# One of two factored-attention batches moves from ahead of a cross attention into the work interleaved with it

## Chip, cores, metric

One core of one Trainium2 chip. The metric is the device time of the whole program in microseconds, the median of several runs. The engines are called PE (TensorE matmul), PEld (its weight load), DVE (VectorE), ACT (ScalarE), POOL (GpSimd) and SP (SyncE, which issues most DMAs).

## What is computed

A decoder of four layers on x of 8 batches, 256 tokens and width 128, with a context of 512 tokens a batch. Each layer adds an attention, a cross attention and a feed-forward part to x, each on the layer-normed x. The change touches the passage from layer 1's feed-forward part (L1_ffn) over layer 2's attention (L2_attn) to layer 2's cross attention (L2_xattn):

```python
x = x + L1_ffn(layernorm(x))
x = x + L2_attn(layernorm(x))
x = x + L2_xattn(layernorm(x), ctx)

def L2_attn(x):                       # 16 heads of width 8
    q, k, v = heads(x @ W_qkv + b_qkv)
    s = q @ k.T * scale
    s = where(fenwick_mask, s, -inf)  # a query sees the keys 0, 1, 2, 4, ... 128 tokens back
    return merge(softmax(s) @ v) @ W_proj + b_proj

def L2_xattn(q, kv):                  # 16 heads of width 8, 256 queries, 512 keys
    qh, kh, vh = heads(q @ Wq.T + bq), heads(kv @ Wk.T + bk), heads(kv @ Wv.T + bv)
    return merge(softmax(qh @ kh.T * scale) @ vh) @ Wo.T + bo

def L1_ffn(x):
    xr, xk = mix(x, previous token's x)
    return sigmoid(xr @ W_r.T) * (relu(xk @ W_k.T) ** 2 @ W_v.T)
```

## The kernel before

The kernel is written against a tile framework: a scheduler orders each engine's instructions by program order as priority and by its own idea of durations, and sets all waits. Only matmuls and transposes issued through the `_Heads` object (lines 451 and 454) keep strict program order among themselves on PE.

x lives in SBUF as 16 tiles of 128 tokens, two a batch; `E.xt(b)` is the layer-normed, transposed x of batch b.

**The factored attention** `_l2_attn` (L2_attn) works on one tile at a time, with a product per offset instead of a full score matrix. `weigh(t)` makes q (`fa_q`), for pairs of offsets keys and values (`fa_kvps`), the products (`fa_pr`, DVE), the value copies (`fa_v`, ACT), the softmax over offsets (`fa_sc`, `fa_red`), and the weighted values (POOL). `apply(t)` sums them (`fa_o`), transposes, multiplies by the output matrix (`fa_yps`), adds to x, and after the second tile of a batch norms that batch (`_norm`, `_normed`). It is a generator: each `yield` is the end of one step. A first tile's `weigh` has 5 steps and a second tile's 6; `apply` has 1 and 5. `through(g, n, ahead)` runs the tiles of n groups of four, `weigh(t)` before `apply(t - 1)`; `ahead(g)` is run before a group's first tile, and is a unit of L1_ffn (7 steps).

**The middle** `_middle` runs L0_ffn to L2_attn. L1_ffn's group 0 is done in its first part. Then comes, at its end, the passage of the change: `E.beginning` of the cross attention is advanced once (fills of the first head buffers on ACT, line 368; the key projection of batch 0, its spread by DMA, and the values); `_run(fa(0, 1))` runs tiles 0 to 3, that is batches 0 and 1; `E.beginning` is advanced again (the query projection `mh_qps` of batch 0, its copy `mh_qf` at line 417, its split `mh_qp` on POOL, eight SP DMAs that spread it over the heads, and the fills of the second head buffers). The rest, `rest()`, becomes the guest: tiles 4 to 15 with L1_ffn's groups 1 to 3 ahead of them, and then the preparation of L2_ffn's weights (10 steps).

**The cross attention** `_heads_attention` runs 128 heads (t, 16 a batch) in one loop. Head t's scores (`mh_sps`) and their maxima (`mh_nm`) are made at t, its exponentials (`mh_e`) 8 heads later, and every four heads are combined. At head 6 of a batch the next batch's keys are projected, at head 9 its queries; before that the loop makes sure that the next batch is normed:

```python
while h == (2 if causal else 9) and b + 1 not in normed_already:
    visit(1)
...
if guest:
    visit(pace(t))
```

`visit(rate)` adds to a credit and runs that many whole steps of the guest. `known` holds the batches normed before the loop begins. Two PSUM banks (`E.heads.g`) serve the guest and the attention's small matmuls.

Of the kernel before, what the change touches and what calls it, by code (L numbers as in the profile page):

```python
# [43 lines left out]
NT = B * S // P  # L44
# [162 lines left out]
def _normed(E, b, z, psum, turn_over=None):  # L207

    ps = psum.tile([P, 2, D], F32, tag="g", name="ln_ps")
    for q in range(2):  # L210
        if turn_over:
            turn_over(ps[:, q, :], z[:, q, :])
        else:
            E.nc.tensor.transpose(ps[:, q, :], z[:, q, :], E.ident)
    E.nc.scalar.copy(E.xt(b), ps.rearrange("p q t -> p (q t)"))  # L215
# [6 lines left out]
def _run(steps):  # L222
    for _ in steps:
        pass
# [544 lines left out]

def _l2_xattn(E, ctx):  # L770
    guest, E.guest = E.guest, None
    _heads_attention(E, ctx, guest=guest, known=(0, 1), pace=lambda t: 1.25)


def _l3_attn(E, ctx):
# [303 lines left out]
def _l2_attn(E, ctx):  # L1079


    nc, W = E.nc, E.w("L2_attn")
    wk = ctx.enter_context(E.tc.tile_pool(name="fa", bufs=2))
    scale = DH ** -0.5
    NO = len(OFFS)
    heads = lambda a: a.rearrange("p (h d) -> p h d", d=DH)
    st = {}

    def weigh(t):
        b, half = divmod(t, 2)  # L1090
        at = slice(half * P, half * P + P)
        if half == 0:
            E.pre_add(b, W("bo"))
        offs = [o for o in OFFS if o < P * (half + 1)]
        no = len(offs)
        ps = E.banks.fa.tile([P, D], F32, tag="g", name="fa_qps")
        E.mm(ps, E.xt(b)[:, at], W("wqkv")[:, :D], start=True, stop=True)
        q = wk.tile([P, D], F32, name="fa_q")
        nc.vector.tensor_tensor(q, ps, W("b")[:, :D], ALU.add)

        yield
        qb = wk.tile([P, D], F32, tag="fa_s", name="fa_qb")
        nc.gpsimd.tensor_tensor(qb, q, W("b")[:, D : 2 * D], ALU.mult)
        pr = wk.tile([P, NO, D], F32, name="fa_pr")
        v = wk.tile([P, NO, D], F32, name="fa_v")
        for i in range(0, no, 2):
            n = min(2, no - i)
            ps = E.banks.fa.tile([P, 2, 2 * D], F32, tag="g", name="fa_kvps")
            for j in range(n):
                E.mm(ps[:, j, :], E.xt(b, offs[i + j])[:, at], W("wqkv")[:, D:], start=True, stop=True)  # L1110
            nc.vector.tensor_tensor(
                pr[:, i : i + n, :], ps[:, :n, :D], q.unsqueeze(1).to_broadcast([P, n, D]), ALU.mult
            )
            nc.scalar.copy(v[:, i : i + n, :], ps[:, :n, D:])
            yield
        sb = wk.tile([P, H], F32, name="fa_sb")
        nc.vector.tensor_reduce(sb, heads(qb), AX.X, ALU.add)
        sc = wk.tile([P, NO, H], F32, name="fa_sc")
        a = sc[:, :no, :]
        nc.vector.tensor_reduce(a, pr[:, :no, :].rearrange("p o (h d) -> p o h d", d=DH), AX.X, ALU.add)  # L1120
        nc.vector.tensor_tensor(a, a, sb.unsqueeze(1).to_broadcast([P, no, H]), ALU.add)
        if half == 0:
            nc.vector.tensor_tensor(a, a, W("fenwick")[:, :no].unsqueeze(2).to_broadcast([P, no, H]), ALU.add)
        red = wk.tile([P, H], F32, name="fa_red")
        wide = red.unsqueeze(1).to_broadcast([P, no, H])
        nc.vector.tensor_reduce(red, a.rearrange("p o h -> p h o"), AX.X, ALU.max)
        nc.vector.tensor_tensor(a, a, wide, ALU.subtract)
        nc.scalar.activation(a, a, AF.Exp, scale=scale)
        nc.vector.tensor_reduce(red, a.rearrange("p o h -> p h o"), AX.X, ALU.add)
        nc.vector.reciprocal(red, red)  # L1130
        nc.vector.tensor_tensor(a, a, wide, ALU.mult)
        v4 = v[:, :no, :].rearrange("p o (h d) -> p o h d", d=DH)
        nc.gpsimd.tensor_tensor(v4, v4, a.unsqueeze(3).to_broadcast([P, no, H, DH]), ALU.mult)

        nc.gpsimd.tensor_tensor(v[:, :4, :], v[:, :4, :], v[:, 4:8, :], ALU.add)
        st[t] = v, no

    def apply(t):
        v, no = st.pop(t)
        o = wk.tile([P, D], F32, tag="fa_s", name="fa_o")  # L1140
        nc.vector.tensor_tensor(v[:, :2, :], v[:, :2, :], v[:, 2:4, :], ALU.add)
        nc.vector.tensor_tensor(o, v[:, 0, :], W("b")[:, 2 * D :], ALU.add)
        nc.vector.tensor_tensor(o, o, v[:, 1, :], ALU.add)
        if no > 8:
            nc.vector.tensor_tensor(o, o, v[:, 8, :], ALU.add)
        ps = E.banks.fa.tile([P, P], F32, tag="g", name="fa_tps")
        E.turn_over(ps, o)
        ot = wk.tile([P, P], F32, name="fa_ot")
        nc.scalar.copy(ot, ps)
        yield  # L1150
        ps = E.banks.fa.tile([P, D], F32, tag="g", name="fa_yps")
        E.mm(ps, ot, W("wo"), start=True, stop=True)
        nc.vector.tensor_tensor(E.x[:, t, :], ps, E.x[:, t, :], ALU.add)
        if t % 2:
            z = _norm(E, t // 2)
            yield
            yield
            yield
            _normed(E, t // 2, z, E.banks.ln, E.turn_over)
            yield t // 2  # L1160

    def through(g, n, ahead=lambda g: ()):

        first, end = 4 * g, 4 * (g + n)
        for t in range(first, end + 1):
            if t < end:
                if t % 4 == 0:
                    yield from ahead(t // 4)
                yield from weigh(t)
            if t > first:  # L1170
                yield from apply(t - 1)

    return through
# [8 lines left out]
def _middle(E, names, then):  # L1182

    nc = E.nc
    plain_pe(E)
    banks = lambda to, name, bufs, side="left": to.enter_context(
        E.tc.tile_pool(name=name, bufs=bufs, space=PSUM, side=side)
    )  # L1190
    if names != MIDDLE:
        for n in names:
            with ExitStack() as scope:
                pg = E.mid_ln = banks(scope, "mid_pg", 6)
                E.banks = SimpleNamespace(fa=pg, rk=pg, ln=pg)
                unit = {
                    "L0_ffn": _l0_ffn, "L1_attn": _l1_attn, "L1_xattn": _l1_xattn, "L1_ffn": _l1_ffn,
                    "L2_attn": _l2_attn,
                }[n](E, scope, *([pg] if n in MIDDLE[:3] else []))
                if n == "L2_attn":  # L1200
                    _run(unit(0, 4))
                    continue
                for g in range(4):
                    _run(unit(g) or ())
        E.close_weights()
        return
    last, psum, scope, early = (ExitStack() for _ in range(4))
    E.mid_ln = banks(psum, "mid_ln", 1)
    mid = banks(scope, "mid_pg", 4, "right")
    moe = _l0_ffn(E, scope, banks(early, "moe_pg", 3))  # L1210
    ra, xa = _l1_attn(E, scope, mid), _l1_xattn(E, scope, mid)
    rk = _l1_ffn(E, scope, "right")
    E.banks = SimpleNamespace(rk=mid, ln=E.mid_ln)
    for s in range(4):
        if s > 2:
            _run(rk(s - 3))
        if s > 1:
            xa(s - 2)
        if s:
            ra(s - 1)  # L1220
        moe(s)
    early.close()
    E.close_big()
    ra(3)
    xa(2)
    xa(3)
    scope.close()
    E.banks.fa = banks(psum, "fa_pg", 3)
    fa = _l2_attn(E, last)
    guest = then in HEADS  # L1230
    begun = E.beginning(then)
    if guest:
        next(begun)
    _run(fa(0, 1))
    if guest:
        next(begun, None)
    psum.close()

    def rest():
        if guest:  # L1240
            g = E.heads.g
            E.mm, E.turn_over, E.transpose = E.heads.mm, E.heads.turn_over, E.heads.transpose
            E.banks = SimpleNamespace(fa=g, rk=g, ln=g)
        with ExitStack() as own:
            if not guest:
                g = banks(own, "mid_pg2", 6)
                E.banks = SimpleNamespace(fa=g, rk=g, ln=g)
            yield from fa(1, 3, _l1_ffn(E, own))
        last.close()
        E.close_weights()  # L1250
        if guest:
            yield from _l2_ffn_weights(E, E.heads.g)

    E.guest = rest()
    if not guest:
        _run(E.guest)
# [499 lines left out]
```

## Time and profile before

| what | us |
|---|---|
| median of three runs | 1811.19 |
| lowest and highest | 1810.04, 1814.04 |
| the profiled execution's own time | 1812.43 |
| its span, first to last instruction | 1810.6 |
| mean granted PE clock | 0.914 |

The span is what the profile explains; some 2 us lie around it. Busy time is a mean over stages with different limits, so a stage has to be read by itself. Where things stand in the span: the factored attention's tiles 0 to 3 have their output matmuls (`fa_yps`) at 852.0, 873.8, 889.7 and 896.9 us, the first scores of the cross attention come at 909.2, its last exponential at 1299.7, and the guest's last step, the weights of L2_ffn, ends near 1238.6. The DMA queue of SP issues the four key spreads of batch 0 from 872.79 and the eight query spreads from 902.70 (5.31 us in all).

### The profile page before, as it was taken

The numbers are of one execution on the slowest core, as the hardware profiler recorded it, in microseconds if no ns is written. First come the engines' busy times: TensorE is split into PE (matmuls) and PEld (weight loads), VectorE is DVE, ScalarE is ACT, GpSimd is POOL, SyncE is SP. The second block draws the span as 40 slices with busy tenths as digits, with TensorE's granted clock in tenths as the row PEclk, the third lists the DMA queues.
The fourth block names the chain that finished last, engine by engine and source line by source line (L and its number), as shares of the span: only waits on it lengthen the run. The fifth ranks groups of instructions, "written<-read, shape, count | busy, mean of one in ns | idle before, by whom it ended". The sixth has DMA issues, their size and how long they took to land. (4 is left out here: it accounts for less than half of the span.)

```text
span 1810.6 us, 29331 instructions
## 1 busy us (share of the span) xinstructions
PE 1485.5 (82%) x10141; PEld 1069.0 (59%) x10141; DVE 1136.2 (63%) x3845; ACT 891.7 (49%) x1822; POOL 501.6 (28%) x998
## 2 busy tenths in 40 slices
PE   5689999999989989777378888879837799789976
PEld 3456677766655556354256665646516677677753
DVE  4567666665636676777377777666466555455555
ACT  7245445555642345222635556456644456466631
POOL 3122222222101121333323433331113433344331
PEclk9799999999989999897689999989967899899996
DMA  4011101114000000000111111011002321111100
GB/s 151 12 36 35 26 14 37 35 32 159 9 1 1 1 1 1 0 1 1 26 43 35 36 29 34 14 36 44 11 18 54 99 54 45 51 49 49 29 1 24
DMA packets 47236, 60.43 MB, mean 33 GB/s; under 512 B 5232, under 2 KB 36976, under 8 KB 46448
## 3 DMA queue, kind: packets, MB, share of 16 engines
q1 hardware_dynamic: 44720, 56.99, 11.9%
q8 instruction: 80, 1.31, 0.3%
q10 hardware_dynamic: 2368, 1.57, 0.3%
q14 instruction: 68, 0.56, 0.1%
HBM read 14.50 MB, written 1.05 MB: 9 GB/s over the span
## 5 line engine op out<-in xcount | busy, mean ns | idle before, releaser
L451 PE MATMUL mh_sps<-mh_k,mh_q 96*128 96x512 f32 (+2 forms) x1024 | 323.5, 398 | 48.2 <-DMA mh_q<-mh_qp 23.9
L451 PE MATMUL mh_bsps<-mh_q,mh_k 128*128 128x256 f32 (+1 forms) x1536 | 354.9, 337 | 7.0 <-ACT mh_e L587 4.1
L587 ACT ACTIVATE mh_e<-mh_bsps 128x512 f32<-128x512 f32 x512 | 280.9, 600 | 119.6 <-PE mh_bsps L451 112.4
L451 PEld LDWEIGHTS mh_bsps<-mh_q,mh_k 128*128 128x128 f32 x1536 | 267.8, 199 | 32.3 <-issue 6.7
L451 PEld LDWEIGHTS mh_sps<-mh_k,mh_q 96*128 96x128 f32 x1024 | 173.3, 203 | 94.9 <-issue 46.9
L514 DVE CUSTOM_DVE_ANT_0 mh_rest<-mh_sps,mask_b 128x512 bf16<-128x512 f32 x256 | 167.1, 684 | 80.9 <-PE mh_sps L451 77.6
L451 PE MATMUL mh_ops<-mh_e,mh_v 128*32 128x256 f32 (+1 forms) x3072 | 204.9, 380 | 11.9 <-ACT mh_e L574 10.6
L533 DVE TENSOR_REDUCE mh_nm<-mh_sps 128x1 f32<-128x512 f32 x256 | 165.0, 680 | 36.9 <-PE mh_sps L451 36.4
L451 PEld LDWEIGHTS mh_ops<-mh_e,mh_v 128*32 128x32 f32 x3072 | 97.5, 113 | 85.0 <-ACT mh_e L574 21.1
L574 ACT ACTIVATE mh_e<-mh_bsps 128x384 f32<-128x384 f32 x256 | 117.2, 493 | 53.5 <-PE mh_bsps L451 30.9
L197 POOL TENSOR_SCALAR ln_rstd<-ln_mv 128x2 f32<-128x2 f32 x96 | 22.0, 229 | 404.6 <-DVE ln_mv L195 404.2
L514 DVE CUSTOM_DVE_ANT_0 mh_rest<-mh_sps,km_q 128x128 bf16<-128x128 f32 (+1 forms) x256 | 80.0, 350 | 66.2 <-PE mh_sps L451 64.5
L540 POOL CAST mh_hi<-mh_nm 128x8 fp32r<-128x8 f32 x128 | 24.8, 194 | 338.9 <-DVE mh_nm L514 203.0
L514 DVE CUSTOM_DVE_ANT_0 mh_rest<-mh_sps,causal 128x128 bf16<-128x128 f32 (+1 forms) x256 | 79.4, 352 | 54.5 <-PE mh_sps L451 51.8
L215 ACT COPY xt<-ln_ps 128x256 f32<-128x256 f32 x96 | 36.1, 376 | 128.3 <-PE ln_ps L454 65.9
L451 PE MATMUL mh_bsps<-mask_t,ident 128*128 128x512 bf16 x256 | 98.8, 386 | 0.4 <-ACT mh_e L587 0.4
L617 ACT COPY mh_osb<-mh_ops 128x256 f32<-128x256 f32 x128 | 47.6, 372 | 89.3 <-PE mh_ops L451 89.1
L552 ACT CAST mh_m<-mh_mps 8x256 fp32r<-8x256 f32 x128 | 46.1, 360 | 91.0 <-PE mh_mps L454 89.6
L882 ACT ACTIVATE moe_si<-moe_gps 128x512 f32<-128x512 f32 x64 | 38.0, 597 | 101.9 <-PE moe_gps L880 81.1
L880 PE MATMUL moe_ups<-xt,w_L_ffn 128*128 128x512 f32 x128 | 69.6, 626 | 6.9 <-ACT moe_si L882 4.8
L201 DVE TENSOR_SCALAR ln_z<-x,ln_mv,ln_rstd 128x128 f32<-128x128 f32 x128 | 41.9, 368 | 50.5 <-POOL ln_rstd L198 50.5
L891 PEld LDWEIGHTS moe_dps<-w_L_ffn,moe_act 128*128 128x128 f32 x512 | 64.1, 199 | 15.9 <-issue 7.7
(359 smaller groups left out, 3098.3 us busy)
## 6 DMA issues: line engine op xcount, KB each, us to landing
mh_k<-mh_kp SPq DMA_DIRECT2D x64, 256.0 KB
mh_q<-mh_qp SPq DMA_DIRECT2D x256, 64.0 KB
mh_k<-mh_kp SPq DMA_DIRECT2D x64, 128.0 KB
w_L_ffn<-in_w_L_ffn SPq DMA_DIRECT2D x2, 1558.0 KB
w_L_attn<-in_w_L_attn SPq DMA_DIRECT2D x2, 1056.0 KB
ctx_t<-in_ctx_t SPq DMA_DIRECT2D x4, 512.0 KB
mh_q<-mh_m ACTq DMA_DIRECT2D x128, 8.0 KB
w_L_ffn<-in_w_L_ffn SPq DMA_DIRECT2D x2, 687.0 KB
```

Of the source, the lines that this page charges most:

```text
L201: (engine or nc.vector).tensor_scalar(z[:, q, :], E.x[:, 2 * b + q, :], mv[:, q, 0:1], rstd[:, q : q + 1], ALU.subtract, ALU.mult)
L215: E.nc.scalar.copy(E.xt(b), ps.rearrange("p q t -> p (q t)"))
L451: return self.E.tc.keep_in_program_order(self.E.nc.tensor.matmul(*a, **kw))
L514: nc.vector.tensor_tensor_reduce(rest[:, : scores.shape[1]], scores, lowered, -1.0, -FLOOR, ALU.add, ALU.min, accum_out=at)
L533: nc.vector.tensor_reduce(u.nm[:, c, col], ps, AX.X, ALU.max, negate=True)
L552: nc.scalar.copy(m, ps[:8].rearrange("p c q -> p (c q)"))
L574: nc.scalar.activation(e, ps, AF.Exp, scale=scale)
L587: nc.scalar.activation(e, ps, AF.Exp, scale=scale)
L617: nc.scalar.copy(osbs[b][:, u4 % 2, :], ops)
L880: nc.tensor.matmul(ps, W("w13")[:, o : o + P], xt, start=True, stop=True)
L882: nc.scalar.activation(si, pgate, AF.Silu)
L891: nc.tensor.matmul(ps[:, t, :], act[:, c, t * P : t * P + P], W("w2")[:, o : o + P], start=c == 0, stop=c == 1)
```

## The change

The unit of `through` becomes tiles instead of groups of four. Only tiles 0 and 1 (batch 0) run between the two advances of the cross attention's beginning; the guest begins with tiles 2 and 3 (batch 1), then L1_ffn's group 1 and tile 4, as before. `known` falls back to its default `(0,)`, and the pace is 2.0 steps for each of the first nine heads and 1.3 after that, where it was 1.25. The other two edited calls are on paths that run when not all layers are asked for, or when no attention follows.

```diff
 def _l2_xattn(E, ctx):
     guest, E.guest = E.guest, None
-    _heads_attention(E, ctx, guest=guest, known=(0, 1), pace=lambda t: 1.25)
+    _heads_attention(E, ctx, guest=guest, pace=lambda t: 2.0 if t < 9 else 1.3)
...
-    def through(g, n, ahead=lambda g: ()):
-
-        first, end = 4 * g, 4 * (g + n)
+    def through(first, end, ahead=lambda g: ()):
+
         for t in range(first, end + 1):
             if t < end:
                 if t % 4 == 0:
...
-                    _run(unit(0, 4))
+                    _run(unit(0, NT))
...
-    _run(fa(0, 1))
+    _run(fa(0, 2 if guest else 4))
...
-            yield from fa(1, 3, _l1_ffn(E, own))
+            yield from fa(2 if guest else 4, NT, _l1_ffn(E, own))
```

## The prediction

> **What bounds the kernel now.** I read the page first, then the busy time by stretch around the second cross attention, then the timeline of those stretches. The page says that TensorE carries the span, so only stretches where it idles can be shortened.
>
> ```profile
> span 1810.6 us, 29331 instructions
> ...
> PE 1485.5 (82%) x10141; PEld 1069.0 (59%) x10141; DVE 1136.2 (63%) x3845; ACT 891.7 (49%) x1822; POOL 501.6 (28%) x998
> ...
> PE   5689999999989989777378888879837799789976
> ```
>
> The 3 in its slice 20 (860 to 905 us) is where the factored attention's first tiles run alone before the cross attention. Busy time by stretch there (columns: window, its length, busy time and instructions of PE, PEld, DVE, ACT, POOL, granted clock, DMA share, GB/s):
>
> ```profile
> 859.00:872.00 13.00, 4.71 (x25) 3.25 (x24) 5.52 (x17) 12.32 (x7) 1.23 (x3) 0.82 0.00 0
> 872.00:881.00 9.00, 5.48 (x17) 3.92 (x18) 4.08 (x14) 5.96 (x10) 7.10 (x8) 0.69 0.50 117
> 881.00:901.00 20.00, 6.58 (x19) 4.14 (x18) 8.48 (x24) 9.64 (x12) 4.98 (x5) 0.59 0.00 0
> 901.00:909.00 8.00, 0.70 (x2) 0.00 (x0) 0.00 (x0) 0.73 (x2) 1.24 (x3) 0.50 0.24 61
> 909.00:933.00 24.00, 18.35 (x62) 12.40 (x63) 17.95 (x41) 6.67 (x11) 7.12 (x15) 0.73 0.11 28
> 933.00:982.00 49.00, 42.91 (x307) 31.98 (x305) 37.42 (x92) 27.23 (x63) 17.34 (x26) 0.93 0.15 34
> ```
>
> From 872 to 909 no engine is half busy; the attention's first nine heads (909 to 933) keep PE and DVE at 75%; after that PE is at 88%. The timeline names the chain (start, length, instruction, idle time before it):
>
> ```profile
> 870.76 0.74 ACT L368 COPY mh_v<-plain 128x668 f32<-128x668 f32 x1
> ...
> 873.46 0.29 ACT L1149 COPY fa_ot<-fa_tps 128x128 f32<-128x128 f32 x1
> ...
> 874.64 0.29 DVE L1153 TENSOR_TENSOR x<-fa_yps,x 128x128 f32<-128x128 f32 x1
> ...
> 880.40 0.37 ACT L215 COPY xt<-ln_ps 128x256 f32<-128x256 f32 x1 [3.02 <-PE ln_ps L1179]
> ...
> 881.07 3.60 ACT L368 CAST mh_k<-plain 2x4096 fp32r<-2x4096 f32 x1
> ...
> 896.90 0.80 PE L1152 MATMUL fa_yps<-w_L_attn,fa_ot 128*128 128x128 f32 x2 [0.35 <-ACT fa_ot L1149]
> ...
> 900.64 1.06 PE L451 MATMUL mh_qps<-xt,w_L_xattn 128*128 128x256 f32 x2
> ...
> 901.74 0.47 ACT L417 ACTIVATE mh_qf<-mh_qps,w_L_xattn 128x256 f32<-128x256 f32 x1 [0.48 <-PE mh_qps L451]
> ...
> 909.24 2.34 PE L451 MATMUL mh_sps<-mh_k,mh_q 96*128 96x512 f32 x4 [7.54 <-DMA mh_q<-mh_qp]
> ```
>
> ACT's four fills of the first head buffers end at 871.5; only then does tile 1's output leave (873.46), and batch 0 is normed at 880.40. Its query projection (900.64) still stands behind batch 1, tiles 2 and 3. From its copy (901.74) to the first scores (909.24), split, eight SP DMAs and their landing take 7.50 us.
>
> **The change part by part.** All sums are against this execution (span 1810.6 us, its time 1812.43); the difference is then applied to the median of the three runs, 1811.19.
>
> *Removed from ahead: tiles 2 and 3.* Tile 1's copy no longer queues behind tile 2's three value copies and exponential: from 873.46 to 872.46, 1.0 us. Norm 0's scale (L197, at 878.27) waited for tile 2's POOL products; without them it follows its statistics, some 3.6 us sooner. So xt of batch 0 is ready near 876.8 (bounds 876 to 880.8: both gains and a little, or none), the query copy 0.85 us later as at 900.89 to 901.74, and the scores 7.50 us after that: 885.2, a gain of 24.0 us. Against it: the second buffers' four fills (3.60, 3.60, 3.63, 0.79 us, 11.6 in all) lay under tiles 2 and 3 and now have less cover. ACT started one just after xt at 881.07; one there would hold the query copy up to 3.1 us and leave 20.9. All of them ahead of it end at 872.75 + 11.6 + 0.4, so 884.8 and scores at 892.3: 16.9. I take 21.5: most of one fill, because the order shown puts one exactly there. Ends 17 and 24.
>
> *Added to the guest: the same tiles.* Guest steps (one per yield): weigh 5 or 6, apply 1 or 5, an FFN unit 7. Before: 133 in all; 12 of them by head 9 (10 x 1.25). After: 150; batch 1 is normed at step 29 (5+6+1+7+5+5). Heads 0 to 8 give 18, so head 9's loop runs the other 11 at once. Behind head 9, 121 steps are left in both kernels, at 1.3 a head rather than 1.25: I cost that at nothing, the heads' own work being the cover; the guest would only end about four heads sooner. So the price falls wholly in heads 0 to 9.
>
> Per tile from the groups between 934 and 1184 us (11 tiles): PE 51.0/11 (fa_kvps) + 0.4 + 0.5 + 0.3 = 5.8; DVE 1.7 products, 1.3 reduction, 1.4 five narrow operations, 0.75 two reductions, 0.55 first sum, 1.4 the rest = 7.1; POOL 2.1 + 1.3 + 0.4 = 3.8; ACT 2.1. Two tiles and a norm: PE 12.2, DVE 15.8, POOL 9.3, ACT 4.6. These issue no DMA; SP's queue keeps its order, with batch 1's query spread behind the burst. ACT and POOL take theirs in idle time (ACT 6.67, POOL 7.12 of 24 us busy). DVE and PE don't. If both filled their idle 6 us, the cost would be 15.8 - 6.0 = 9.8; at DVE's present 75% it is 15.8/0.75 = 21. The cadence gives a third figure: projections of batches 1 to 7 run from 933.0 to 1241.6, 51.4 us per 16 heads with 20 steps; after the guest's end, 1242 to 1300 holds 46 score reductions (23 heads) and 61 exponentials (30.5), about 2.2 us a head, 35 per 16. A step costs (51.4-35.2)/20 = 0.81, and 17 cost 13.8. I take 15, between cadence and DVE.
>
> *The wait that the burst adds.* The last four steps are batch 1's norm and nothing else, and TensorE takes head 9's projection and scores in program order behind it, with ACT's exponentials waiting on those. The same chain ahead took 900.64 - 896.90 = 3.7 us from output matmul to projection, 0.8 us for the copy before: 4.5. It costs nothing where DVE is behind anyway. I take 2; ends 0 and 4.5.
>
> The row for the clock: mh_sps took 676 ns each in 909 to 933 (granted 0.73) and 456 later. The Trainium skill, "TensorE: Matmul & The Clock Gate", Part 1, says that the array drops to half rate after about 3.4 us of idling and needs as long a busy stretch to recover. By that rule the burst's wait would also slow the next 3.4 us, an estimated 1.7 us more, and the sum would be -2.8; the rows show the slow start but no drop in mid-attention, where waits are shorter.
>
> **Sum:** -21.5 + 15 + 2 = -4.5 us, so 1811.2 - 4.5 = 1806.7.
>
> **Rivals.**
>
> 1. *The burst takes the place of the wait removed: slower.* Place: heads 5 to 9. At two steps a head tile 2's transpose comes six steps, three heads, after its last products: 3 x 2.67 (24/9) = 8.0 us, while from last product to transpose (885.86 to 896.07) took 10.2. TensorE stands 2.2 us there, 4.5 at head 9, and DVE never fills its idle time (21): 27.7 against 20.9, +6.8, so 1818. For it: in-order PE and 75% DVE. Against: at 1.25 steps no such wait shows. It decides from the point at which first scores to batch 1's projection, 24 us now, take more than 45.
> 2. *The start absorbs the work.* Idle PE and DVE are filled (9.8), no burst wait, no fill in front (24.0): -14, so 1797. For it: 25% idle in both. Against: that idling is waiting in order, not want of work.
> 3. *The change doesn't bring the query projection forward as far as it says.* All fills go ahead (16.9 gained, 17 paid): 0, so 1811. For it: ACT ran fills back to back from 863.64.
>
> **How the numbers follow.** Chances: forecast 0.46, rival 1 0.27, rival 2 0.12, rival 3 0.15. Its own range, by gain 19 to 24 and cost 13 to 19: 1800 to 1811. The full range reaches to rival 2 and rival 1: 1797 to 1819. A measurement here can tell about 0.2% (3.6 us) from no change. Faster by more (under 1807.6): 0.36 of the forecast's 0.46, rival 2, a little of rival 3: 0.49. Within: 0.10 of the forecast, 0.10 of rival 3 and 1: 0.20. Slower: 0.31, rival 1 and the tail of 3.
>
> **What would show it.** mh_qps of batch 0 at 877 to 879 (right) or near 884 (rival 3); first mh_sps 17 to 24 us sooner; from there to batch 1's mh_qps about 41 us (forecast), under 36 (rival 2), over 45 (rival 1); a TensorE gap of 2 to 4 us before ln_ps and mh_qps at head 9. I am wrong if the schedule elsewhere moves, or if batches 2 to 7's cadence leaves 51 us by more than 1.

## The result, and the profile after

The changed kernel takes 1821.17 us (median of four runs, 1819.46 to 1823.12) against 1810.62 us for the kernel before in the same session (four runs, 1809.68 to 1814.04): ratio 1.005, 95% interval 1.0031 to 1.0069. It is slower by some 10.5 us, above the top of the predicted range. The profiled execution took 1819.46 us, 7.0 more than the one of before.

The page of the changed kernel, its span, PE's busy time, and PE's busy share and granted clock by slice:

```profile
span 1817.7 us, 29289 instructions
...
PE 1485.1 (82%) x10103; PEld 1070.5 (59%) x10141; DVE 1137.4 (63%) x3845; ACT 894.5 (49%) x1822; POOL 502.6 (28%) x998
...
PE   5689999999989989767478788878846789789986
...
PEclk9799999999989999896689899989956999899997
```

PE is busy as long as before (1485.1 against 1485.5 us); the 7.1 us of span are idle time. The 3 in slice 20 (863 to 909 us here) has become no more than a 4, although the attention's heads now begin inside that slice, and slice 23 (1000 to 1045 us) has fallen from 8 to 7. Split at marks that both traces have (the first scores, the query projections of batches 1 and 7, L2_ffn's first gate matmul, `qf_gps`):

| stretch | before, us | after, us | difference | predicted |
|---|---|---|---|---|
| start to first scores | 909.2 | 889.3 | -19.9 | -21.5 |
| first scores to batch 1's projection | 23.8 | 50.6 | +26.8 | +17 |
| batch 1's projection to batch 7's | 308.5 | 313.2 | +4.7 | 0 |
| batch 7's projection to L2_ffn | 73.7 | 72.0 | -1.7 | 0 |
| L2_ffn to the end | 495.4 | 492.6 | -2.8 | 0 |

**The front** went nearly as predicted. The timeline of ACT, then that of PE, in the changed kernel:

```profile
877.74 0.37 ACT L215 COPY xt<-ln_ps 128x256 f32<-128x256 f32 x1 [0.43 <-PE ln_ps L1178]
878.13 3.60 ACT L368 CAST mh_k<-plain 2x4096 fp32r<-2x4096 f32 x1
881.76 0.47 ACT L417 ACTIVATE mh_qf<-mh_qps,w_L_xattn 128x256 f32<-128x256 f32 x1
```

```profile
878.16 1.22 PE L451 MATMUL mh_qps<-xt,w_L_xattn 128*128 128x256 f32 x2 [0.46 <-ACT xt L215]
889.29 1.19 PE L451 MATMUL mh_sps<-mh_k,mh_q 96*128 96x512 f32 x2 [9.90 <-DMA mh_q<-mh_qp]
```

Batch 0's projection comes at 878.16 instead of 900.64. One fill (878.13, 3.60 us) stands between xt and the query copy at 881.76, the one that the working allowed for, and from the copy to the scores it is again 7.5 us.

In the 9 us before the scores PE does nothing at all (first line below): that is what is left of the fill, and the spread's wait, which the change leaves at 7.5 us.

**The first heads** are where the forecast failed. Busy time by stretch after (window, length, PE, PEld, DVE, ACT, POOL, granted clock, DMA share, GB/s):

```profile
880.00:889.00 9.00, 0.00 (x0) 0.00 (x0) 0.00 (x0) 6.35 (x4) 1.12 (x2) 0.50 0.21 55
...
889.30:939.90 50.60, 32.74 (x112) 23.07 (x112) 35.19 (x94) 13.65 (x30) 16.76 (x24) 0.80 0.09 21
889.30:989.50 100.20, 75.59 (x416) 55.15 (x416) 71.70 (x179) 39.27 (x88) 34.87 (x52) 0.87 0.11 27
```

and from the kernel before, first scores to batch 2's projection:

```profile
909.20:981.90 72.70, 61.17 (x367) 44.28 (x367) 55.37 (x132) 33.90 (x73) 24.36 (x41) 0.87 0.13 32
```

Up to batch 2's projection, where both kernels have done 25 heads, the stretch is 27.5 us longer: PE is busy 14.4 us more, and idle 24.6 us instead of 11.5, 13.1 us more. So the added work filled none of the idle time; it brought its own. PE's own timeline shows with what:

```profile
909.44 0.45 PE L454 MATMUL fa_tps<-ident,fa_o 128*128 128x128 f32 x1 [4.02 <-DVE fa_o L1143]
...
924.21 0.66 PE L454 MATMUL ln_ps<-ident,ln_z 128*128 128x128 f32 x2 [4.80 <-DVE ln_z L201]
...
938.77 0.69 PE L454 MATMUL ln_ps<-ident,ln_z 128*128 128x128 f32 x2 [3.00 <-DVE ln_z L201]
939.93 0.78 PE L451 MATMUL mh_qps<-xt,w_L_xattn 128*128 128x256 f32 x1 [0.46 <-ACT xt L215]
```

The brackets give the idle time and who ended it. The first wait is that of tile 2's transpose for its sums, the second that of a norm which L1_ffn's unit makes (the kernel before has that one too, 4.29 us), the third that of batch 1's norm at head 9. The clock falls after each of them. The same stretch cut at the waits:

```profile
905.40:909.40 4.00, 0.03 (x1) 0.00 (x0) 3.69 (x10) 0.27 (x1) 2.44 (x2) 0.98 0.00 0
909.40:913.40 4.00, 3.96 (x10) 2.22 (x11) 1.07 (x4) 1.64 (x4) 2.25 (x2) 0.59 0.01 2
...
919.40:924.20 4.80, 0.01 (x1) 0.02 (x1) 4.08 (x15) 0.00 (x0) 0.95 (x2) 0.87 0.41 76
924.20:928.50 4.30, 2.60 (x10) 2.02 (x10) 2.17 (x9) 3.12 (x5) 2.92 (x4) 0.50 0.02 4
928.50:935.50 7.00, 6.50 (x18) 4.91 (x19) 3.17 (x10) 1.65 (x5) 0.41 (x1) 0.67 0.00 0
935.50:940.00 4.50, 0.97 (x5) 0.43 (x4) 3.48 (x13) 0.69 (x3) 1.66 (x3) 1.00 0.00 0
940.00:944.00 4.00, 4.00 (x15) 3.37 (x16) 1.78 (x5) 1.43 (x3) 3.67 (x4) 0.58 0.01 2
944.00:950.00 6.00, 6.00 (x37) 5.23 (x39) 5.80 (x13) 4.01 (x9) 1.48 (x5) 1.00 0.33 87
```

Each of these three waits is followed by a stretch at about half the clock: 0.59 after the first, 0.50 and 0.67 after the second, 0.58 after the third, and only then 1.00. After the first and the third PE has work all the time: in 940 to 944, 4.00 us of busy PE at 0.58 lose 4.00 x 0.42 = 1.7 us. Such a wait costs its length and some 1.7 us more. The kernel before has stretches at half clock too: by the clock records of the two traces PE is busy at half clock for 18.5 us up to batch 2's projection before and for 23.5 us after, so the slower clock makes 2.5 of the 27.5 us.

### The profile page after: what moved, and what is told of

It is laid out like the page before. It is cut to its first block, busy times and chain, and to the rows that moved or that the text cites. A ratio compares the mean times of both kernels' runs of the same rounds, so it can differ in the third digit from the quotient of the medians.

```text
span 1817.7 us, 29289 instructions
## 1 busy us (share of the span) xinstructions
PE 1485.1 (82%) x10103; PEld 1070.5 (59%) x10141; DVE 1137.4 (63%) x3845; ACT 894.5 (49%) x1822; POOL 502.6 (28%) x998
## 5 line engine op out<-in xcount | busy, mean ns | idle before, releaser
L451 PE MATMUL mh_sps<-mh_k,mh_q 96*128 96x512 f32 (+2 forms) x1024 | 321.5, 396 | 53.4 <-DMA mh_q<-mh_qp 27.4
L540 POOL CAST mh_hi<-mh_nm 128x8 fp32r<-128x8 f32 x128 | 24.7, 193 | 317.4 <-DVE mh_nm L514 199.4
L451 PE MATMUL mh_bsps<-mask_t,ident 128*128 128x512 bf16 x219 | 84.7, 387 | 0.4 <-ACT mh_e L587 0.4
L451 PE MATMUL fa_kvps<-w_L_attn,xt 128*128 128x256 f32 x238 | 68.6, 422 | 8.3 <-DVE x L1153 4.4
```

What stands on the lines that cost most here:

```text
L451: return self.E.tc.keep_in_program_order(self.E.nc.tensor.matmul(*a, **kw))
L540: nc.gpsimd.tensor_copy(hi, nm)
```

## The experiments

Each was compared with the kernel before on the same chip. "Change" in a figure is median minus median of that comparison; ratios carry their 95% interval. Diffs are against the changed kernel, except where another is named.

**1. Is the gain in front real, and does it reach the end?** The changed kernel without tiles 2 and 3, at the pace of before:

```diff
-            yield from fa(2 if guest else 4, NT, _l1_ffn(E, own))
+            yield from fa(4, NT, _l1_ffn(E, own))
...
-    _heads_attention(E, ctx, guest=guest, pace=lambda t: 2.0 if t < 9 else 1.3)
+    _heads_attention(E, ctx, guest=guest, known=(0, 1), pace=lambda t: 1.25)
```

> Leaves tiles 2 and 3 (batch 1's factored attention) out altogether, with the old pace of 1.25 and batch 1 taken as normed: the front of the change alone. First scores near 889 in both theories (909 before). If the loss lies in heads 0 to 9 alone, whether by waits (theory W) or by plain work (theory L), the 20 us gained ahead reach the end: 1790 to 1793, and first scores to batch 1's projection stay near 24 us. If the gain is lost again later whatever the guest does, 1797 or more.

1793.29 against 1813.07 us, -19.8; 0.9888 (0.9858 to 0.9918). First scores at 888.9 us, batch 1's projection 24.0 us after them. The 20 us won in front come out whole at the end: nothing later swallows them.

**2. Are the added steps dear without batch 1's deadline?** Tiles 2 and 3 run ahead as before *and* a second time as the guest's first work, so batch 1 is normed in time and nothing has to be run ahead of its projection:

```diff
-    _run(fa(0, 2 if guest else 4))
+    _run(fa(0, 4))
...
-    _heads_attention(E, ctx, guest=guest, pace=lambda t: 2.0 if t < 9 else 1.3)
+    _heads_attention(E, ctx, guest=guest, known=(0, 1), pace=lambda t: 2.0 if t < 9 else 1.3)
```

> Keeps tiles 2 and 3 ahead as before and runs them a second time as the guest's first work at the changed kernel's pace, so batch 1's projection waits for none of it; x of batch 1 gets their contribution twice. First scores stay near 909. Theory L (the work costs it): the whole span gains about as much as first scores to batch 1's normed second pass do in the changed kernel, +25 us or more over before, 1836 and up. Theory W (the waits of the deadline cost half of it): +12 to +18 us, 1823 to 1829, because the 11 steps spread over heads 9 to 17 and no projection waits at head 9.

1843.76 against 1813.07 us, +30.7; 1.0167 (1.0143 to 1.019). From first scores to batch 1's projection 35.2 us, to batch 2's 96.5:

```profile
915.10:1011.60 96.50, 72.51 (x407) 51.93 (x407) 68.52 (x172) 39.05 (x87) 31.25 (x49) 0.84 0.12 28
```

PE is idle 24.0 us in it, as in the changed kernel (24.6). The deadline has only moved on, though: by the pace and the order of the steps, 38 of the 46 steps up to batch 2's norm are done when batch 2's projection is due, so the other 8 run as a burst ahead of it, and PE waits for that norm:

```profile
1010.28 0.84 PE L454 MATMUL ln_ps<-ident,ln_z 128*128 128x128 f32 x2 [3.29 <-DVE ln_z L201]
```

The two experiments add up: -19.8 + 30.7 = +10.9, where the change gave +10.5. The intervals reach 4 to 5 us to either side, so that so close an agreement is partly luck. The profiles agree with it all the same: from the first scores to the end this kernel takes 26.4 us longer than the one before, and the changed kernel 27.0. (The first scores come at 915.1 us here, 5.9 later than before; 4.0 of these are there already at L1_ffn's first matmul, 681.2 against 677.2 us, far ahead of the passage.) The change is a gain in front of 20 and a price of the moved steps of 27 to 30.

**3. Does spreading the burst help?** 3.3 steps a head do all 29 steps before head 9:

```diff
-pace=lambda t: 2.0 if t < 9 else 1.3
+pace=lambda t: 3.3 if t < 9 else 1.3
```

> The changed kernel with 3.3 steps instead of 2.0 for each of the first nine heads, so that batch 1 is normed by head 8 and no burst is left. If the burst at head 9 is the dear part of W: first scores to batch 1's projection 51 -> 42 to 45 us, 1812 to 1816. If instead the chains are just as exposed when steps stand closer, or under theory L: 48 to 54 us, 1818 to 1825.

1822.46 against 1813.07 us; 1.005 (1.0028 to 1.0071), the ratio of the change itself; 49.9 us to batch 1's projection. No burst is left, but the waits are: 4.21 us at tile 2's transpose, 6.48 and 1.85 at the norms that L1_ffn's unit makes, and at batch 1's norm

```profile
937.76 1.01 PE L454 MATMUL ln_ps<-ident,ln_z 128*128 128x128 f32 x2 [3.02 <-DVE ln_z L201]
```

So it is not the burst that costs.

**4. Can part of the steps go into the hole ahead of head 0's scores?** Eleven steps are run just before the loop over the heads (`lead` is a new argument):

```diff
+    visit(lead)
...
-    _heads_attention(E, ctx, guest=guest, pace=lambda t: 2.0 if t < 9 else 1.3)
+    _heads_attention(E, ctx, guest=guest, lead=11, pace=lambda t: 2.0 if t < 9 else 1.3)
```

> The changed kernel with the first 11 guest steps (both weigh parts) ahead of head 0's scores, while TensorE waits for batch 0's query spread; no burst is left (11 + 18 = 29 steps by head 9). Theory W: some 6 to 9 us of the idle 9.9 us are filled and the burst's wait goes, batch 1's projection at 922 to 930 instead of 940, 1803 to 1811. Theory L: only the filled idle time is won, 1812 to 1816. If the second buffers' fills on ACT block the value copies until 886, the steps move behind them and little is won: 1816 to 1821.

1824.26 against 1813.07 us; 1.0062 (1.0041 to 1.0083), above all that was expected. The stretch to batch 1's projection fell to 42.5 us, but the first scores came at 895.9 instead of 889.3, so that batch 1's projection comes at 938.3 instead of 939.9 us. The value copies of the tiles stand on ACT behind its fills, and PE, in order, behind those.

**5. The later rate in the changed kernel.** I had costed 1.3 against 1.25 at nothing.

```diff
-pace=lambda t: 2.0 if t < 9 else 1.3
+pace=lambda t: 2.0 if t < 9 else 1.25
```

> The changed kernel with 1.25 steps a head after the ninth, as before the change, instead of 1.3. The 4 us that batches 2 to 7 take longer in the changed kernel: if the faster rate makes them, 1816 to 1819; if they come from how the schedule falls, 1819 to 1824.

1815.36 against 1813.4 us; 1.0012 (1.0003 to 1.0022), below the change's interval: the rate is worth some 7 us (0.0038 of 1811), give or take 4 by the two intervals (1.9 between the two profiles, counted from the first scores). A difference of 4.4 us shows in one place, batch 2's projection to batch 3's: 56.4 us in the changed kernel, 52.0 here. POOL's timeline of the changed kernel there:

```profile
1035.02 1.96 POOL L1133 TENSOR_TENSOR fa_v<-fa_v,fa_sc 128x1024 f32<-128x1024 f32 x1 [0.54 <-DVE fa_sc L1131]
1036.94 1.26 POOL L420 TENSOR_TENSOR mh_kp<-mh_kf,mh_kp 128x512 fp32r<-128x512 f32 x1
1038.16 1.26 POOL L1135 TENSOR_TENSOR fa_v<-fa_v 128x512 f32<-128x512 f32 x1
1039.39 0.22 POOL L197 TENSOR_SCALAR ln_rstd<-ln_mv 128x2 f32<-128x2 f32 x1
```

```profile
1040.88 0.73 PE L454 MATMUL ln_ps<-ident,ln_z 128*128 128x128 f32 x2 [4.72 <-DVE ln_z L201]
```

and of this kernel:

```profile
1034.80 0.22 POOL L197 TENSOR_SCALAR ln_rstd<-ln_mv 128x2 f32<-128x2 f32 x1 [1.19 <-DVE ln_mv L195]
...
1036.49 2.00 POOL L1133 TENSOR_TENSOR fa_v<-fa_v,fa_sc 128x1024 f32<-128x1024 f32 x1 [0.66 <-DVE fa_sc L1131]
```

At 1.3 a tile's wide products (1.96 and 1.26 us, with a key split between) fall ahead of batch 3's norm on POOL, a 0.22 us operation; it runs 4.5 us after its statistics, and PE waits 4.72 us. At 1.25 the norm goes first.

**6. The pace alone, in the kernel before** (the diff is against that).

```diff
-known=(0, 1), pace=lambda t: 1.25
+known=(0, 1), pace=lambda t: 2.0 if t < 9 else 1.3
```

> The kernel before with only the pace of the change (2.0 for nine heads, 1.3 after): no work added, 7 guest steps pulled from the steady stretch into the first nine heads. Theory P (place: a step among the first heads costs far more than one in the steady stretch, since the exponentials, 8 heads behind, give no cover yet): first scores to batch 1's projection 24 -> 33 to 36 us, and of that 3 to 8 us stay at the end, 1815 to 1820. Theory U (a step costs the same anywhere, 0.8 us): the first heads lengthen by 6 us and the rest shortens by as much, 1810 to 1813.

1821.02 against 1813.4 us, +7.6; 1.0042 (1.0028 to 1.0056). With not one step added, the pace costs nearly three quarters of what the whole change loses: 31.3 us to batch 1's projection, 55.5 from there to batch 2's.

**7. The even rate of 1.3 alone, in the kernel before.**

```diff
-known=(0, 1), pace=lambda t: 1.25
+known=(0, 1), pace=lambda t: 1.3
```

> The kernel before with an even 1.3 steps a head instead of 1.25; nothing else changed. Theory R (the later rate is dear by itself: at 1.3 the guest's norms fall behind POOL's wide products and TensorE waits in order): most of the 7.6 us that the change's pace cost on the kernel before, so 1816 to 1820. If it is the dense start (2.0 for nine heads) that cost them: 1811 to 1815.

1808.52 against 1812.61 us, -4.1; 0.9968 (0.9957 to 0.9979). So the theory that 1.3 is dear by itself falls, and what cost experiment 6 its 7.6 us is the dense start: 1.0042 against 0.9968. It is lower than either expectation. Batch 2's projection to batch 3's takes 56.0 us here too, with the same wait for batch 3's norm (4.71 us); the four intervals from batch 1's projection to batch 5's lose 9.8 us in sum against the kernel before, and the last two win 11.9 (48.8 and 49.0 us against 52.5 and 57.2), where the guest runs out sooner. In the changed kernel the last two are 50.7 and 53.4 us: there the loss in the middle is not won back.

**8. The same 17 steps in the steady stretch.** Tiles 2 and 3 ahead, and a second time between tiles 7 and 8, at an even pace chosen to end the guest at about the same head. The diff is against the kernel before, and `through` takes a list of tiles here:

```diff
-known=(0, 1), pace=lambda t: 1.25
+known=(0, 1), pace=lambda t: 1.41
...
-            yield from fa(1, 3, _l1_ffn(E, own))
+            yield from fa((4, 5, 6, 7, 2, 3, 8, 9, 10, 11, 12, 13, 14, 15), _l1_ffn(E, own))
```

> The kernel before with tiles 2 and 3 run a second time, as in the run with both, but between tiles 7 and 8, in the attention's steady stretch, at an even 1.41 steps a head so that all 150 steps end at the same head; x of batch 1 gets their contribution twice. Theory P: the same 17 steps cost 11 to 16 us there, 1823 to 1829 against 1844 for the run that has them first. Theory U: 25 us or more again, 1836 and up.

1832.97 against 1813.4 us, +19.6; 1.011 (1.0095 to 1.0124). 1.15 us a step, where the cadence had given 0.81; the time lies between the two that were expected.

**9. The same steps first, at the same even pace.**

```diff
-pace=lambda t: 2.0 if t < 9 else 1.3
+known=(0, 1), pace=lambda t: 1.41
...
-    _run(fa(0, 2 if guest else 4))
+    _run(fa(0, 4))
```

> The kernel before with tiles 2 and 3 run a second time as the guest's first work, at the even 1.41 steps of the run that had them between tiles 7 and 8; x of batch 1 gets their contribution twice. Against that run (20 us over before) only the place differs. If the place at the start is dear: 5 us or more above it, 1838 and up. If a step costs the same anywhere: within 4 us of it, 1829 to 1837.

1843.35 against 1812.61 us, +30.7; 1.0165 (1.0151 to 1.0179). As dear as at two steps a head, and 11 us dearer than the same steps later. Batch 1's projection comes 24.7 us after the first scores, as before, and the next interval is 70.2 us: the bill only moves on. So does the deadline, by the count of steps: 11 of them run as a burst ahead of batch 2's projection.

**10. Moving only the ends of the tiles.** `weigh(2)` and `weigh(3)` stay ahead, after batch 0's projection and spread were issued; their `apply` parts (six steps) become guest work behind L1_ffn's group 1, at 1.7 steps a head, then 1.25:

```diff
-    _run(fa(0, 2 if guest else 4))
+    _run(fa(0, 2))
+    if guest:
+        next(begun)
+    for t in (2, 3):
+        _run(fa.weigh(t))
     if guest:
         next(begun, None)
...
-            yield from fa(2 if guest else 4, NT, _l1_ffn(E, own))
+            ffn = _l1_ffn(E, own)
+            yield from ffn(1)
+            for t in (2, 3):
+                yield from fa.apply(t)
+            yield from fa(4, NT, lambda g: ffn(g) if g > 1 else ())
```

> A third arrangement: tiles 0 and 1 whole, then batch 0's projection and spread, then only the weigh parts of tiles 2 and 3 ahead, under the spread; their apply parts (6 steps instead of 17) are the guest's work right after the FFN unit, 13 steps to batch 1's norm, at 1.7 steps for nine heads and 1.25 after. If the price goes by the steps moved: first scores some 17 to 20 us sooner than before, 6 steps at 1.1 us in return and no burst, 1796 to 1804. If the start is dear however little is moved: 1806 to 1813.

1816.13 against 1812.61 us, +3.5; 1.0017 (1.0007 to 1.0028), above both expectations. The first scores came at 890.3, but after three of them PE stood again:

```profile
900.97 0.80 PE L451 MATMUL mh_sps<-mh_k,mh_q 96*128 96x512 f32 x1 [9.72 <-DVE mh_nm L533]
```

9.72 us, as long as the wait for the spread that it was to do without: DVE worked on tiles 2 and 3 first and came to these scores' maxima only at 900.23. Batch 1's projection came 35.2 us after the first scores. An early first score is no early second one.

**11. Keeping both batches ahead, and only issuing batch 0's projection and spread before tiles 2 and 3**, with the second fills last and the pace of 1.25:

```diff
-    _run(fa(0, 2 if guest else 4))
+    _run(fa(0, 2))
+    if guest:
+        next(begun)
+    _run(fa(2, 4))
     if guest:
         next(begun, None)
...
-            yield from fa(2 if guest else 4, NT, _l1_ffn(E, own))
+            yield from fa(4, NT, _l1_ffn(E, own))
...
+            yield
             for f in fills[4:]:
                 f()
```

> Both batches ahead and the old pace, but batch 0's query projection and spread are issued right after batch 0 is normed, before tiles 2 and 3, whose work then lies under the projection, the split and the spread's landing; the second buffers' fills come after tile 3. If the front gain can be had without the guest's price: batch 0's projection at 877 to 880, first scores when tile 3 lets its PSUM banks go, 899 to 903 instead of 909, 24 us to batch 1's projection as before, 1802 to 1806. If the scores still come at 909 or a fill or a bank holds tile 3 longer: 1809 to 1814.

1809.25 against 1813.4 us, -4.2; 0.9976 (0.9959 to 0.9992). Far from 20 us: PE still takes tiles 2 and 3 before the scores.

**12. That, at the even rate of 1.3** (against experiment 11).

```diff
-known=(0, 1), pace=lambda t: 1.25
+known=(0, 1), pace=lambda t: 1.3
```

> The kernel with both batches ahead, batch 0's query projection and its spread issued before tiles 2 and 3 (measured about 4 us under the kernel before), with the even pace of 1.3 steps a head (by itself also about 4 us under it). If the two gains are independent, they add: about -8, ratio 0.9955. If one is a matter of how the guest's steps happen to fall on the heads, which the earlier start shifts again, the sum is something else: anything from -4 to +4, ratio 0.998 to 1.002. The first interval, scores to batch 1's projection, is expected at 23 to 25 us in either case.

1805.93 against 1812.79 us, -6.9; 0.9963 (0.995 to 0.9976). The first scores came at 906.9 us, right behind batch 1's norm, and batch 1's projection 24.1 us later. It beats both kernels, and so does experiment 7 (0.9968); the intervals overlap, so that the hoist adds to the rate isn't shown.

## Why the prediction was wrong

**Removed from ahead, -21.5: right.** -19.9 in the profile, -19.8 at the end (experiment 1), within the ends of 17 and 24. The choice of one fill in front of the query copy was right to the instruction. Of the two gains ahead of it only one came: tile 1's copy left at 873.41 us, as before (873.46), and xt of batch 0 was made 2.7 us sooner (877.74), not 4.0.

**Added to the guest, +15: the step that failed.** With batch 1's deadline taken away the same 17 steps cost 30.7 us, at two steps a head (experiment 2) and at an even pace (9); from the first scores on, in the profiles, 26.4 and 27.3. The DVE figure (15.8) counted one engine's work and let PE's 12.2 run beside it, the waits unchanged; the runs refute that. From first scores to batch 2's projection PE's busy time grew by 14.4 us, near the 12.2 us of work that I had counted plus the 2.5 that the slower clock adds, and its idle time by 13.1 on top. Of these 13.1, 4.0 end at tile 2's transpose and 3.8 at norms, 3.0 of them at batch 1's. PE pays such waits because these matmuls keep program order. I had written as much as the argument against rival 2 ("that idling is waiting in order, not want of work") and then not used it in my own sum. (Not every chain brings a wait: tile 3's transpose, at 934.60 us, follows tile 4's matmuls without one.) The cadence figure failed for a second reason: the 0.81 us a step is a difference of two averages, and measured directly in the steady stretch a step costs 1.15 (19.6/17, experiment 8). (The 12 steps that I counted by head 9 before took in head 9's own; 11 come before its projection. That is one step.)

The other 11 us go with the place, by experiments 8 and 9; from the first scores on, in the profiles, they are 7.6 (27.3 against 19.7). The two differ also in their bursts: by the count of steps 11 and 2 ahead of the projections of batches 2 and 3 in experiment 9, and 7 and 2 ahead of those of batches 4 and 5 in 8. Experiment 6 has no added step and no burst: there seven steps brought forward lengthen the stretch from first scores to batch 2's projection by 14.1 us, and 7.6 stay at the end. That stretch in nine kernels, with two counts of steps from the pace and the order of the steps:

| kernel | tile steps before head 9 | all guest steps before batch 2's projection | us |
|---|---|---|---|
| before | 4 | 31 | 72.7 |
| even 1.3 (7) | 4 | 32 | 72.9 |
| second time later (8) | 5 | 35 | 79.6 |
| before with the dense start (6) | 11 | 38 | 86.8 |
| ends of the tiles moved (10) | 8 | 35 | 93.3 |
| second time first, even (9) | 12 | 46 | 94.9 |
| second time first, dense (2) | 12 | 46 | 96.5 |
| changed | 22 | 49 | 100.2 |
| 3.3 steps a head (3) | 22 | 50 | 102.7 |

Both counts give the order, but for experiment 10 with its wait of 9.72 us. By the second, experiments 7 and 10 aside, each step over 31 costs 1.5 to 2.0 us here, where the forecast had 15/17 = 0.9.

The first fits a reading by which a tile's chains are dearest in the first nine heads, where the exponentials have not begun and PE has little besides scores to put between a chain's steps. That reading is argued, not shown: the number of steps in the stretch as a whole orders the kernels as well, and no run moved the exponentials.

**The wait that the burst adds, +2: seen, but no term of its own.** PE waits 3.00 and 0.46 us at head 9, inside the ends of 0 and 4.5. But experiment 3, which has no burst, has the same wait at that norm (3.02 us) and is no cheaper. So the wait belongs to the added chain, and its price to that of the steps.

**The clock** was weighed and set aside, because the rows showed "no drop in mid-attention". That reading was too coarse: means over 24 and 49 us hide it. Cut at the waits, the clock is at 0.58 or 0.59 for some 4 us after the first and the third and at 0.50 to 0.67 for some 11 us after the second, and in 940 to 944 it loses 1.7 us, just what the estimate by the Trainium skill's "TensorE: Matmul & The Clock Gate", Part 1, had put there. That page asks for an idle window of about 3.4 us; here waits of 3.00 and 0.46 us with a transpose between them were enough.

**The later rate, 0: wrong in both directions.** 1.3 costs some 7 us, give or take 4, in the changed kernel (experiment 5) and gains 4 in the kernel before (7). POOL's order ahead of batch 3's norm is seen at 1.3 in both (waits of 4.72 and 4.71 us), so it does not explain the difference; why the last intervals win the loss back in the one kernel and not in the other stays open. The average interval of the changed kernel, 52.2 us, is 1.2 off the 51 that my sign of being wrong names and 0.8 off the 51.4 measured before: too near the bound of 1 to be a warning.

**Rival 1** gave the better number: it wanted more than 45 us up to batch 1's projection (50.6) and 1818. Its first wait is there too, 4.0 us at tile 2's transpose where it said 2.2. But its point, that the burst at head 9 decides, is not borne out: without a burst the time is no shorter (experiments 3 and 4), and with the deadline moved on to batch 2 the bill is still 30.7. So its number was partly luck. **Rival 2** is contradicted by the idle time, and **rival 3** by batch 0's projection at 878.16.

## What to carry over

Idle time that comes from waiting in order is no room: before pricing work into it, look at what ended each idle time, and count the new work at its full time on the in-order engine plus the waits that its chains bring. The gain of a move is measured by leaving the moved work out and its price by running it twice, in the old place and the new; then look whether a deadline has only moved on. A rate of interleaving that looks like a detail can move the time by several us, either way, and is to be tried by itself, in both kernels.

## What was not expected of the hardware

The clock drops after shorter waits than the prediction had allowed for. In the kernel of experiment 8 waits of 0.98 and 2.05 us, with one matmul between them, are enough:

```profile
969.90:973.40 3.50, 0.56 (x2) 0.19 (x1) 3.12 (x7) 0.70 (x2) 2.87 (x3) 0.99 0.00 0
973.40:976.80 3.40, 3.32 (x26) 2.11 (x30) 2.50 (x6) 1.46 (x3) 2.55 (x5) 0.50 0.02 5
976.80:980.20 3.40, 3.06 (x31) 1.91 (x24) 1.84 (x4) 0.37 (x1) 0.38 (x1) 1.00 0.00 0
```

PE works for 0.56 of 3.50 us, and then has 3.32 us of work in 3.40 us at a clock of 0.50. In the clock records of thirteen of the fourteen traces (all but experiment 11's, whose upper step is 0.95) the clock is either full or half and changes only at marks 3.41 us apart. After a unit of that length at full clock in which PE's matmuls were busy for less than 40%, the next unit was at half in all 303 cases; after one busy for 70% or more, in 22 of 4625, all at two places of the program; between the two, in 168 of 650. So PE's share of a unit decided here, not one unbroken wait.
